# Setup of a cross-attention and expert kernel: query weights turned by transpositions, context loaded first

## The chip, the cores and the metric

The kernel runs on one core of a Trainium2 chip. The metric is the device time of one execution in microseconds, lower being better. One core has five engines that run side by side and meet only at semaphores: PE (TensorE, matrix products, with its weight loads listed as PEld), DVE (VectorE), ACT (ScalarE), POOL (GpSimd) and SP (SyncE, which here only starts transfers). All data are 32-bit floats.

## The reference

```python
x = x + xattn(ctx_1024, layernorm(x), fside, fside, ln1_w, ln1_b, ln2_w, ln2_b, Wq, Wkv, Wout)
x = x + ffn(layernorm(x), Wr, Wg, Wu, Wd)          # 9 experts, the best 2 for each token

def xattn(x, latents, shift, scale, ln1_w, ln1_b, ln2_w, ln2_b, Wq, Wkv, Wout):   # x: the context
    xn, ln = layernorm(x, ln1_w, ln1_b), layernorm(latents, ln2_w, ln2_b)
    q = ln @ Wq                                     # 16 heads of 64
    k, v = split(xn @ Wkv, 2)
    q = q * (1 + scale) + shift                     # one number for each batch and head
    attn = softmax(q . k / 8)                       # over the 77 context rows
    return (attn @ v) @ Wout
```

The input `x` is 4 x 1024 x 256, the context 4 x 77 x 256, `Wq` 256 x 1024, `Wkv` 256 x 2048, `fside` 4 x 16. The second layer norm has a weight `ln2_w` and an offset `ln2_b` for each of the 256 channels.

## The kernel before

The kernel has three stretches: a setup (to about 72 us in the trace), the attention of 32 groups of 128 tokens, and the experts. Only the setup is touched by the change. It folds everything that depends on the context alone into two tables, so that the attention needs no query projection. For each head, `g` = (query weights of the head) times (keys of the head): scores are then one product of normalised tokens with `g`. `u` does the same for values and `Wout`.

The schedule is manual (`tc.manual_schedule()`): each engine executes its instructions in the order of the program text. What is written first on an engine goes first, and an instruction that waits holds up all behind it on that engine. PSUM is used through `bank_tile`, which hands out eight banks in turn, so a product waits until the product eight places earlier has been read out. `evict(k, dst, src)` reads a bank out with DVE for odd k and with ACT for even k.

The setup's order around the change, with `P` = 128, `C` = 2 halves of the 256 channels, `NP` = 8 pairs of heads, `B * J` = 4 x 77 = 308 context rows:

- Lines 345 to 347: `qrows`, the two rows `ln2_w` and `ln2_b`, loaded from ACT's queue.
- Lines 367 to 374, SP's queue: `wq_sb` in four quarters of 256 KB with the context `cx` (308 KB) between the second and the third, then `wk_sb`, `wv_sb`, `wo_sb` of 1 MB each.
- Lines 376 to 389, POOL's queue: `cw`, `cb` (the weight and offset of the context's layer norm), `fs` (`fside` on all partitions), the router's weights, and the filling of `list_d` in DRAM.
- Lines 394 to 415: `fold`, a 256 x 256 matrix that is nearly diagonal. It holds `ln2_w` on the diagonal, and it also carries a subtraction of the last channel and the column of `ln2_b`, so that one product with it turns the query weights over (channels from partitions to the free dimension), scales them, and puts the offsets' product into the last column.
- Lines 417 to 427: moments of the context and `cn`, the normalised context, all on DVE but a root.
- `turn_queries(n)`, lines 431 to 438: for each pair of heads two products of `wq_sb` with `fold` into `pwq`, read out to `wqT`, by DVE and ACT in turn. Four pairs come ahead of the context's transpositions into `pct` (line 445, read out to `cT` at line 448 by ACT), four behind.
- Lines 456 to 466: `shift`, `scale1` from `fs`, on DVE.
- Lines 470 to 482: the key products `pk` (line 473), read out twice: to `kT` by ACT (477) and, times `scale1`, to `kTs` by DVE (478).
- Lines 483 to 489: `cfold`, small DVE products with the last column of `wqT`. Lines 493 to 509: the router's weights, with the product `pm`. Lines 535 to 553: small tables of numbers for the lists, on DVE.
- Lines 511 to 559, POOL: clearing of `vbd` (line 512, tied to the end of `normed`, the last write of `cn`), `vrem` and `u` (519, 521), and index patterns.
- Lines 560 to 573: 32 products `pgk` (line 565), one for each head and channel half. The two heads of a pair sit on different halves of the partitions. The first head of each pair is read out by ACT, the second by DVE, in two copies each.
- Lines 574 to 581: the products `pb`. Behind them, `kside` is given back, the first `x` are loaded, and the value side follows (`pwo`, `pv`, `pu`).

Of the kernel before, what the change touches and what calls it, by code (L numbers as in the profile page):

```python
# [8 lines left out]
F32 = mybir.dt.float32  # L9
# [12 lines left out]
def kernel(  # L22
# [319 lines left out]
    with tc.tile_pool(name="vside", bufs=1) as vside, ExitStack() as kvs:  # L342
        kside = kvs.enter_context(tc.tile_pool(name="kside", bufs=1))

        qrows = kside.tile([2, D], F32, name="qrows")
        for k, src in enumerate((ln2_w, ln2_b)):
            nc.scalar.dma_start(out=qrows[k : k + 1, :], in_=src.rearrange("(o d) -> o d", o=1))
# [19 lines left out]
        for k in range(4):  # L367
            if k == 2:
                nc.sync.dma_start(out=cx[:J], in_=ctx_in.rearrange("b j d -> j b d"))
            at = slice(k * quarter, (k + 1) * quarter)  # L370
            nc.sync.dma_start(out=wq_sb[:, :, at], in_=wq_v[:, :, at])
        nc.sync.dma_start(out=wk_sb, in_=wkv[:, :INNER].rearrange("(c p) n -> p c n", p=P))
# [4 lines left out]
        fs = vside.tile([P, B, NP, 2], F32, name="fs")  # L377
        nc.gpsimd.dma_start(
            out=fs.rearrange("p b n t -> p (b n t)"),
            in_=fside.rearrange("(o b) h -> o (b h)", o=1).to_broadcast([P, B * H]),  # L380
        )
# [9 lines left out]

        fold = kside.tile([P, C, D], F32, name="fold")
        minus = kside.tile([P, 1], F32, name="minus")
        nc.vector.memset(fold[:, 0, P:], 0.0)

        pq = bank_tile("pq")
        for c in range(C):
            nc.tensor.transpose(  # L400
                pq[:, 2 * c : 2 * c + 2], qrows[:, c * P : (c + 1) * P], ident[:2, :2]
            )
        qwb = kside.tile([P, C, 2], F32, name="qwb")
        nc.vector.tensor_copy(qwb.rearrange("p c k -> p (c k)"), pq[:, : 2 * C])
        qw = qwb[:, :, 0]
        nc.vector.tensor_scalar(fold[:, 0, :P], ident, qw[:, 0:1], None, ALU.mult)
        nc.vector.tensor_copy(fold[:, 0, D - 1 : D], qwb[:, 0, 1:2])
        nc.vector.scalar_tensor_tensor(
            minus, ident[:, P - 1 : P], -1.0, qw[:, 1:2], ALU.mult, ALU.mult
        )  # L410
        nc.scalar.activation(fold[:, 1, :P], ones, AF.Copy, scale=minus)
        nc.vector.tensor_scalar(
            fold[:, 1, P : D - 1], ident[:, : P - 1], qw[:, 1:2], minus, ALU.mult, ALU.add
        )
        nc.vector.tensor_copy(fold[:, 1, D - 1 : D], qwb[:, 1, 1:2])

        cmv = moments(cx[:J], J, "ctx")
        csd = kside.tile([P, B], F32, name="csd")
        cr = kside.tile([P, B], F32, name="cr")
        nc.scalar.activation(csd[:J], cmv[:J, :, 1], AF.Sqrt, bias=eps_t[:J])  # L420
        nc.vector.reciprocal(cr[:J], csd[:J])
        cn = kside.tile([P, B, D], F32, name="cn")
        for b in range(B):
            normed = nc.vector.tensor_scalar(
                cn[:J, b, :], cx[:J, b, :], cmv[:J, b, 0:1], cr[:J, b : b + 1],
                ALU.subtract, ALU.mult,
            )
        wqT = kside.tile([P, NP, D], F32, name="wqT")
        cT = vside.tile([P, C, B * J], F32, name="cT")

        def turn_queries(n):
            pt = bank_tile(f"pwq{n}")
            for c in range(C):
                nc.tensor.matmul(
                    pt[:, :D], wq_sb[:, c, n * P : (n + 1) * P], fold[:, c, :],
                    start=(c == 0), stop=(c == C - 1),
                )
            evict(n, wqT[:, n, :], pt[:, :D])

        for n in range(NP // 2):  # L440
            turn_queries(n)
        for c in range(C):
            pt = bank_tile(f"pct{c}")
            for b in range(B):
                nc.tensor.transpose(
                    pt[:, b * J : (b + 1) * J], cn[:J, b, c * P : (c + 1) * P], ident[:J, :J]
                )
            nc.scalar.activation(
                cT[:, c, :], pt[:, : B * J], AF.Identity,
                bias=cb[:, c : c + 1], scale=cw[:, c : c + 1],  # L450
            )
        for n in range(NP // 2, NP):
            turn_queries(n)
# [13 lines left out]

        kT = kside.tile([P, NP, B * J], F32, name="kT")
# [14 lines left out]
        for t in range(2):  # L483
            half = slice(64 * t, 64 * t + 64)
            nc.vector.tensor_tensor(
                cfold[half, :, t, :], scale1[half],
                wqT[half, :, D - 1 : D].to_broadcast([64, NP, B]), ALU.mult,
            )
            nc.vector.tensor_tensor(cfold[half, :, t, :], cfold[half, :, t, :], shift[half], ALU.add)
# [10 lines left out]
        pm = bank_tile("pm")  # L500
        for c in range(C):
            nc.tensor.matmul(pm[:, :E], ones, wr_sb[:, c, :], start=(c == 0), stop=(c == C - 1))
        nc.vector.tensor_tensor(
# [48 lines left out]
        for t, half in zip(nowhere, (lower, upper)):  # L552
            nc.vector.tensor_scalar(t, half, float(TOK), None, ALU.mult)
# [914 lines left out]
```

## Time and profile before

| | |
|---|---|
| median of 3 runs | 927.88 us (927.68 to 929.5) |
| the profiled execution's own time | 927.98 us, of which the span is 926.1 us |
| PE busy | 907.6 us, 98% of the span |
| DVE, ACT, POOL busy | 450.4, 339.2, 320.1 us |
| key products `pk` (line 473) | from 15.49, for 8.46 us |
| products `pgk` (line 565) | from 24.22 to 34.48 us |
| first value-side product `pwo` (line 607) | 35.59 us |

All times of single instructions are counted from the start of the span. A timeline line reads: start, time that the group covers, engine, line, operation, output <- inputs, shapes, count, and in brackets how long the engine had been idle before it and what ended the wait. Each product of 32-bit numbers appears as two MATMUL records, a transposition as one. Matmuls are pipelined, so the records overlap, and the distance between starts is the pace. In a table by stretches, each engine has its busy time and the number of instructions, and the last three columns are the clock that PE was granted, the share of the DMA engines, and GB/s.

### The profile page before, as it was taken

The numbers are of one execution on the slowest core, as the hardware profiler recorded it, in microseconds if no ns is written. First come the engines' busy times: TensorE is split into PE (matmuls) and PEld (weight loads), VectorE is DVE, ScalarE is ACT, GpSimd is POOL, SyncE is SP. The second block draws the span as 40 slices with busy tenths as digits, with TensorE's granted clock in tenths as the row PEclk, the third lists the DMA queues.
The fourth block names the chain that finished last, engine by engine and source line by source line (L and its number), as shares of the span: only waits on it lengthen the run. The fifth ranks groups of instructions, "written<-read, shape, count | busy, mean of one in ns | idle before, by whom it ended". The sixth has DMA issues, their size and how long they took to land. (4 is left out here: it accounts for less than half of the span.)

```text
span 926.1 us, 13326 instructions
## 1 busy us (share of the span) xinstructions
PE 907.6 (98%) x4190; PEld 706.7 (76%) x4190; DVE 450.4 (49%) x1330; ACT 339.2 (37%) x1071; POOL 320.1 (35%) x330
## 2 busy tenths in 40 slices
PE   8999999999999999999999999999999999999996
PEld 6676777777777777788887778777777777788885
DVE  5776678788788977753622222222222222222221
ACT  3567465665746565551111222222222211112210
POOL 5000000422504251246544444435435435444422
PEclk9999999999999999999999999999999999999998
DMA  6100010503112610455869779779779777779822
GB/s 211 47 23 1 1 69 24 46 24 46 34 36 69 222 36 24 117 143 157 204 188 305 212 207 308 216 207 308 219 209 311 223 211 217 221 220 308 233 34 23
DMA packets 109785, 136.92 MB, mean 148 GB/s; under 512 B 24251, under 2 KB 79939, under 8 KB 109716
## 3 DMA queue, kind: packets, MB, share of 16 engines
q1 hardware_dynamic: 92303, 118.78, 41.9%
q0 software_dynamic: 17408, 17.30, 10.5%
q8 instruction: 34, 0.56, 0.3%
q14 instruction: 36, 0.29, 0.1%
q10 hardware_dynamic: 4, 0.00, 0.0%
HBM read 119.38 MB, written 18.33 MB: 149 GB/s over the span
## 5 line engine op out<-in xcount | busy, mean ns | idle before, releaser
L1107 PE MATMUL pg<-xT,wgu 128*128 128x256 f32 x1144 | 251.7, 379 | 0.4 <-PEq L1424 0.4
L1107 PEld LDWEIGHTS pg<-xT,wgu 128*128 128x128 f32 x1144 | 215.9, 190 | 29.3 <-issue 0.8
L1181 PE MATMUL po<-wd,hid 128*128 128x256 f32 (+1 forms) x804 | 180.5, 379 | 0.0
L1181 PEld LDWEIGHTS po<-wd,hid 128*128 128x128 f32 (+1 forms) x804 | 147.2, 187 | 21.2 <-issue 0.7
L261 ACT ACTIVATE ex<-psc,mx 128x77 f32<-128x77 f32 x512 | 123.6, 360 | 102.0 <-DVE mx L251 102.0
L1216 POOL DMA_INDIRECT out_dram<-co,ids x63 | 100.7, 1598 | 172.1 <-DVE co L1184 148.3
L832 POOL DMA_INDIRECT list_d<-r_entry,r_pli x64 | 68.3, 1068 | 255.2 <-DVE r_pli L830 125.2
L324 PE MATMUL po<-u,aT 128*128 128x265 f32 x640 | 151.7, 391 | 0.9 <-ACT aT L313 0.6
L247 PE MATMUL psc<-g,zT 128*128 128x462 f32 (+1 forms) x384 | 139.1, 511 | 1.2 <-ACT zT L236 1.2
L324 PEld LDWEIGHTS po<-u,aT 128*128 128x128 f32 x640 | 118.7, 189 | 23.7 <-ACT aT L313 1.8
L1114 DVE TENSOR_TENSOR hid<-pg,sl 128x256 f32<-128x256 f32 x130 | 55.0, 424 | 160.2 <-ACT sl L1113 159.9
L1113 ACT ACTIVATE sl<-pg 128x256 f32<-128x256 f32 x130 | 49.7, 383 | 218.4 <-PE pg L1107 213.4
L247 PEld LDWEIGHTS psc<-g,zT 128*128 128x128 f32 x384 | 72.5, 189 | 59.2 <-issue 49.4
L1184 DVE TENSOR_SCALAR co<-po,ids 128x256 f32<-128x256 f32 x67 | 32.4, 484 | 136.4 <-PE po L1181 136.3
L1065 POOL DMA_INDIRECT yin<-y_d,ids x67 | 70.3, 1049 | 23.7 <-issue 17.3
L251 DVE TENSOR_REDUCE mx<-psc 128x6 f32<-128x462 f32 (+1 forms) x96 | 55.6, 580 | 18.4 <-PE psc L247 15.6
L281 DVE TENSOR_REDUCE sm<-ex 128x16 f32<-128x1232 f32 x32 | 45.9, 1435 | 36.9 <-ACT ex L261 36.3
L313 ACT COPY aT<-pa 128x512 f32<-128x512 f32 (+1 forms) x96 | 49.3, 551 | 27.2 <-PE pa L305 27.2
L305 PEld LDWEIGHTS pa<-ident,an 128*128 128x128 f32 x320 | 36.9, 141 | 7.7 <-PE po L324 1.4
L305 PE MATMUL pa<-ident,an 128*128 128x128 f32 x320 | 40.2, 273 | 1.0 <-DVE an L285 1.0
L285 DVE TENSOR_TENSOR an<-ex,rs 128x1024 f32<-128x1024 f32 x32 | 39.2, 1225 | 1.1
L1169 ACT COPY hid<-ph 128x384 f32<-128x384 f32 x15 | 7.2, 478 | 73.9 <-PE ph L1164 73.9
(305 smaller groups left out, 842.2 us busy)
## 6 DMA issues: line engine op xcount, KB each, us to landing
wgu<-in_L_ffn_Wg_dram SPq DMA_DIRECT2D x41, 704.0 KB
wd<-in_L_ffn_Wd_dram SPq DMA_DIRECT2D x41, 640.0 KB
wgu<-in_L_ffn_Wu_dram SPq DMA_DIRECT2D x41, 512.0 KB
wgu<-in_L_ffn_Wu_dram SPq DMA_DIRECT2D x41, 128.0 KB
x<-in_x_dram SPq DMA_DIRECT2D x8, 512.0 KB
out_dram<-x SPq DMA_DIRECT2D x8, 512.0 KB
y_d<-y SPq DMA_DIRECT2D x8, 512.0 KB
w<-in_L_ffn_Wg_dram SPq DMA_DIRECT2D x5, 704.0 KB
```

Source lines behind the costliest of these rows:

```text
L247: nc.tensor.matmul(psc[:, :w], zT[:, c, :], g_sb[i // NS // GPB][:, c, h * J : h * J + w], start=(c == 0), stop=(c == C - 1),)
L251: nc.vector.tensor_reduce(nmx[i][:, h : h + n], psc[:, : n * J].rearrange("p (h j) -> p h j", h=n), AX.X, ALU.max, negate=True,)
L261: nc.scalar.activation(exs[i][:, h + q, :], pscs[k][:, q * J : (q + 1) * J], AF.Exp, bias=nmx[i][:, h + q : h + q + 1],)
L305: nc.tensor.transpose(pa[:, q * P : (q + 1) * P], ans[i][:, (k + q) * P : (k + q + 1) * P], ident)
L324: nc.tensor.matmul(po[:, :DE], aT[:, n, :], u_sb[b][:, n, :], start=(n == 0), stop=(n == KC - 1))
L832: i = nc.gpsimd.indirect_dma_start(out=list_d[:, :], out_offset=bass.IndirectOffsetOnAxis(ap=place_i[:, s : s + 1], axis=0), in_=entries[k ...
L1065: return nc.gpsimd.indirect_dma_start(out=dst, out_offset=None, in_=src, in_offset=bass.IndirectOffsetOnAxis(ap=offsets, axis=0), **kw,)
L1107: nc.tensor.matmul(pg[:, g, :], w[:, c, at : at + P], xT[:, c, :], start=(c == 0), stop=(c == C - 1),)
L1113: nc.scalar.activation(sl, pg[:, 0, :], AF.Silu)
L1114: nc.vector.tensor_tensor(hid[:, f, :], pg[:, 1, :], sl, ALU.mult)
L1181: nc.tensor.matmul(po[rows, :D], hid[:, f, at], d[:, f, :], start=(f == 0), stop=(f == NF))
L1216: i = nc.gpsimd.indirect_dma_start(out=out_r, out_offset=bass.IndirectOffsetOnAxis(ap=rows_of(j, h, rows), axis=0), in_=cos[j][:, h, :], i ...
```

## The change

Four things are altered, all in the setup.

1. The query weights are turned by 16 plain transpositions (two pairs of heads to a bank) in place of 16 products with `fold`. `ln2_w`, now loaded on all partitions as `wrow`, is multiplied in when DVE reads the bank out (`scale_queries`, 128 x 512 at a time). The first of these comes ahead of `cT`, the other three each follow a key read-out. The subtraction of the last channel becomes eight ACT instructions in place, with `wlast`. `fold` and what built it is gone.
2. The product of the offsets `ln2_b` with the query weights is made by itself: `qb` holds the offsets in one column of 32, and 16 matmul records on four column tiles give `pcq`, which ACT copies to `crow`. `turn_offsets` turns it and makes `cfold`.
3. The context is loaded first, in two halves, ahead of the query weights; the key weights come in four quarters. `wrow` and `fs` are loaded from ACT's queue. Two of the four `cn` go to ACT, one of the two `cT` to DVE.
4. `turn_offsets`, `router_weights` and `numbers` are moved from ahead of the `pgk` loop into it, ahead of its pairs 2, 4 and 6.

```diff
-        qrows = kside.tile([2, D], F32, name="qrows")
-        for k, src in enumerate((ln2_w, ln2_b)):
-            nc.scalar.dma_start(out=qrows[k : k + 1, :], in_=src.rearrange("(o d) -> o d", o=1))
+        wrow = kside.tile([P, D], F32, name="wrow")
+        nc.scalar.dma_start(
+            out=wrow, in_=ln2_w.rearrange("(o d) -> o d", o=1).to_broadcast([P, D])
+        )
+        fs = vside.tile([P, B, NP, 2], F32, name="fs")
+        nc.scalar.dma_start(
...
-        for k in range(4):
-            if k == 2:
-                nc.sync.dma_start(out=cx[:J], in_=ctx_in.rearrange("b j d -> j b d"))
-            at = slice(k * quarter, (k + 1) * quarter)
-            nc.sync.dma_start(out=wq_sb[:, :, at], in_=wq_v[:, :, at])
-        nc.sync.dma_start(out=wk_sb, in_=wkv[:, :INNER].rearrange("(c p) n -> p c n", p=P))
+        for i in range(2):
+            at = slice(i * BH, (i + 1) * BH)
+            nc.sync.dma_start(out=cx[:J, at], in_=ctx_in[at].rearrange("b j d -> j b d"))
+        wk_v = wkv[:, :INNER].rearrange("(c p) n -> p c n", p=P)
+        for dst, src in ((wq_sb, wq_v), (wk_sb, wk_v)):
+            for k in range(4):
+                at = slice(k * quarter, (k + 1) * quarter)
+                nc.sync.dma_start(out=dst[:, :, at], in_=src[:, :, at])
...
-        fs = vside.tile([P, B, NP, 2], F32, name="fs")
-        nc.gpsimd.dma_start(
...
+        qb = kside.tile([P, C, P // QT], F32, name="qb")
+        nc.gpsimd.memset(qb, 0.0)
+        nc.gpsimd.dma_start(out=qb[:, :, 0], in_=ln2_b.rearrange("(c p) -> p c", p=P))
...
-        fold = kside.tile([P, C, D], F32, name="fold")
...
-        nc.vector.tensor_copy(fold[:, 1, D - 1 : D], qwb[:, 1, 1:2])
...
+        cm = kside.tile([P, B], F32, name="cm")
...
+        pwq = []
+        for n in range(0, NP, 2):
+            pt = bank_tile(f"pwq{n}")
+            for k in range(2):
+                for c in range(C):
+                    nc.tensor.transpose(
+                        pt[:, k * D + c * P : k * D + (c + 1) * P],
+                        wq_sb[:, c, (n + k) * P : (n + k + 1) * P], ident,
+                    )
+            pwq.append(pt)
...
+        def scale_queries(k):
+            nc.vector.tensor_tensor(
+                wqT[:, 2 * k : 2 * k + 2, :], pwq[k].rearrange("p (n d) -> p n d", n=2),
+                wrow.unsqueeze(1).to_broadcast([P, 2, D]), ALU.mult,
+            )
...
+        nc.vector.scalar_tensor_tensor(
+            cm[:J], cmv[:J, :, 0], -1.0, cr[:J], ALU.mult, ALU.mult
+        )
         cn = kside.tile([P, B, D], F32, name="cn")
         for b in range(B):
...
+            if b % 2:
+                normed = nc.vector.tensor_scalar(
...
+            else:
+                nc.scalar.activation(
+                    cn[:J, b, :], cx[:J, b, :], AF.Identity,
+                    bias=cm[:J, b : b + 1], scale=cr[:J, b : b + 1],
+                )
+        scale_queries(0)
         for c in range(C):
             pt = bank_tile(f"pct{c}")
...
+            if c:
+                nc.vector.tensor_scalar(
+                    cT[:, c, :], pt[:, : B * J], cw[:, c : c + 1], cb[:, c : c + 1],
+                    ALU.mult, ALU.add,
+                )
+            else:
+                nc.scalar.activation(
...
-        for n in range(NP // 2, NP):
-            turn_queries(n)
...
         for n in range(NP):
             pk = bank_tile(f"pk{n}")
...
+            if n < NP // 2 - 1:
+                scale_queries(n + 1)
+            elif n == NP // 2 - 1:
+                nc.vector.tensor_scalar(
+                    wlast, wqT[:, :, D - 1], -1.0, None, ALU.mult
+                )
+            if n >= NP // 2:
+                for m in (2 * n - NP, 2 * n - NP + 1):
+                    nc.scalar.activation(
+                        wqT[:, m, :], wqT[:, m, :], AF.Identity, bias=wlast[:, m : m + 1]
+                    )
+
+        pcq = bank_tile("pcq")
+        for c in range(C):
+            for q in range(QT):
+                nc.tensor.matmul(
+                    pcq[q * P // QT : (q + 1) * P // QT, :D], qb[:, c, :],
+                    wq_sb[:, c, q * quarter : (q + 1) * quarter],
+                    start=(c == 0), stop=(c == C - 1),
+                )
+        nc.scalar.copy(crow, pcq[:, :D])
+
+        def turn_offsets():
+            pt = bank_tile("pcqt")
+            for k in range(2):
+                nc.tensor.transpose(
+                    pt[:, k * P : (k + 1) * P], crow[:, k * P : (k + 1) * P], ident
+                )
+            nc.vector.tensor_copy(
+                cq.rearrange("p (q k) -> p q k", k=2),
+                pt[:, : 2 * P].rearrange("p (k q r) -> p q k r", k=2, q=QT)[:, :, :, 0],
+            )
...
+        def router_weights():
...
+        def numbers():
...
         for n in range(NP):
+            if n == 2:
+                turn_offsets()
+            if n == NP // 2:
+                router_weights()
+            if n == NP - 2:
+                numbers()
             for c in range(C):
```

## The prediction

> **What bounds the kernel now.** I read the busy table and the slices first.
>
> ```profile
> PE 907.6 (98%) x4190; PEld 706.7 (76%) x4190; DVE 450.4 (49%) x1330; ACT 339.2 (37%) x1071; POOL 320.1 (35%) x330
> ...
> PE   8999999999999999999999999999999999999996
> ```
>
> PE is full from the first slice on (23 us each) to the last. Whatever PE gains in the setup is passed on to the end, one for one, as nothing behind it waits for a fixed moment. So I follow PE's own timeline of the first 36 us:
>
> ```profile
> 4.44 6.46 PE L434 MATMUL pwq<-fold,wq_sb 128*128 128x256 f32 x16 [0.72 <-DVE fold L407]
> 10.74 1.42 PE L445 MATMUL pct<-ident,cn 77*128 77x77 f32 x8
> 11.99 3.66 PE L434 MATMUL pwq<-fold,wq_sb 128*128 128x256 f32 x16
> 15.49 8.46 PE L473 MATMUL pk<-cT,wk_sb 128*128 128x308 f32 x32
> ...
> 24.22 2.86 PE L565 MATMUL pgk<-kTs,wqT 64*128 64x308 f32 x18
> 28.03 6.45 PE L565 MATMUL pgk<-kTs,wqT 64*128 64x308 f32 x46 [0.96 <-DVE g L144]
> 34.42 1.24 PE L577 MATMUL pb<-kT,cfold 128*32 128x308 f32 x16
> 35.59 1.09 PE L607 MATMUL pwo<-ident,wo_sb 128*128 128x128 f32 x8
> ```
>
> The same product takes 6.46 us for the first sixteen records and 3.66 us for the second sixteen. The timeline of single stretches shows two paces:
>
> ```profile
> 6.31 1.06 PE L434 MATMUL pwq<-fold,wq_sb 128*128 128x256 f32 x2
> ...
> 12.25 0.59 PE L434 MATMUL pwq<-fold,wq_sb 128*128 128x256 f32 x2
> ```
>
> The starts are 0.43 us apart in the first and 0.22 in the second. The distance changes at 9.8 us, 5.3 after the first dense product. PE starts slow and becomes twice as fast; the granted clock stands at 1.00 all the while. Next DVE and POOL, from the timelines of these engines:
>
> ```profile
> 7.91 1.40 DVE L163 BATCH_NORM_STATS2 bn_ctx<-cx 77x6 f32<-77x256 f32 x4 [3.01 <-DMA cx<-in_ctx_dram]
> ...
> 15.95 1.94 POOL L521 MEMSET u<- 128x1060 f32 x2
> ...
> 16.03 1.89 DVE L460 COPY shift<-fs 64x32 f32<-64x32 f32 x2
> ...
> 27.36 7.71 DVE L144 COPY g<-pgk 128x154 f32<-128x154 f32 x32
> ```
>
> The context lands only at 7.9. The two tiny copies of 64x32 last 0.94 us each, exactly as long as POOL's two memsets beside them: a copy within SBUF waits for the POOL instruction that is running. And DVE reaches its read-outs of `pgk` at 27.36, as small work holds it from 24.8 on; PE, eight banks ahead, stands still for it before 28.03. Last, the table by stretches for the transfers:
>
> ```profile
> 4.00:5.50 1.50, 1.06 (x3) 0.88 (x4) 0.82 (x5) 0.40 (x1) 1.50 (x3) 1.00 0.51 103
> ...
> 7.00:8.50 1.50, 1.50 (x5) 1.15 (x5) 0.59 (x2) 0.00 (x0) 0.00 (x0) 1.00 1.28 304
> 8.50:9.00 0.50, 0.50 (x3) 0.41 (x2) 0.50 (x3) 0.00 (x0) 0.00 (x0) 1.00 0.71 180
> 10.00:14.00 4.00, 3.92 (x22) 3.03 (x22) 2.21 (x8) 1.93 (x5) 2.40 (x1) 1.00 1.01 412
> ```
>
> Query weights and context are 1.36 MB, with the small loads 1.42. Adding up the GB/s of the half microseconds gives 1.47 MB at 8.5, a part of it the filling of `list_d`. The dip after 8.5 and the rise to 412 mark the passage to the key weights with their longer rows. So the last query quarter lands at about 8.7 now.
>
> **The change part by part.** Counted against the profiled execution: 927.98 us, its span 926.1. That is 0.1 above the median.
>
> *Loads.* Ahead of the last query quarter stand the same bytes, in another order, and 0.13 MB for `wrow`. At the 304 GB/s of the third row this is 0.4 us; where engines stand half idle, as in the first row, it is nothing. Bounds 8.6 to 9.7; I take 9.0. SP issues 12 transfers where it issued 8, at 0.47 us each; the next on its queue is `x` at 35, so this is free. ACT issues two, as before. POOL gives up one issue (0.57) and gets one with a small memset: its last issue at 6.6 still ends ahead of `vbd`, which waits for `cn`. The first key quarter (256 KB, 0.9 us at 1 KB rows) lands at 9.9, about 1.5 us before it is needed; without that cover each microsecond would count in full.
>
> *Up to the key products.* PE's order is: sixteen transpositions, eight of the context, keys. The transpositions replace 10.1 us of PE time. The first twelve follow their quarters; only the last four count. Nearest row: `pwo`, eight in 1.09 us, so 0.12 each at full pace, 0.23 at the slow one: 0.5 to 0.9. The eight of `pct`, whose last five took 0.55 in all, 0.09 apart, cost 0.7 at the slow pace for the four that count; then 0.25 to drain and 0.55 for ACT's `cT`. Keys start at 9.0 + 0.9 + 0.7 + 0.25 + 0.55 = 11.4 at the slow pace, 10.7 at the full one, against 15.49. The context is no longer late: landed by 4 to 6, then 2.7 us of statistics, root and scaling, so `cn` is done by 8.5. If it landed 1.5 us later than that it would set the start. The steps that built `fold` (DVE, 3.8 to 4.9) lay ahead of an idle DVE; taking them out gives nothing.
>
> *The pace.* This decides. 32 key records take 8.46 us at full pace, 0.264 each, and 0.514 at the slow one (times 0.427/0.219). By the trace alone any work could be what brings PE up to speed: PE then counts as busy from the first quarter on (about 6 us), has its 5.3 us at 11.3 and runs the keys at full pace. Against this stands the Trainium skill, "TensorE: Matmul & The Clock Gate", Part 4, PE-mode transpose: transpositions do not count as activity for the clock gate. By Part 1 of that page the switch comes after one full window of about 3.4 us of matmul activity, and windows run freely, so 3.4 to 6.8 us after dense work begins; the 5.3 of the trace lies inside. The change takes away just the dense matmuls that used up the slow time, and hands it to the keys. The skill's rule gives: switch at 11.4 + 5.3 = 16.7, by then 10.3 records; 21.7 more at 0.264 are 5.7; keys end at 22.4 against 23.95, a gain of 1.55. With the switch 3.4 or 6.8 us after the start it is 2.5 or 0.8. The trace's reading leaves PE to be paced by DVE (below), which ends the keys at 21.0, a gain of 2.9. No row shows transpositions on a slow PE, so I take the rule.
>
> *DVE behind `cT`.* The shift work of 16.03 to 18.88 comes at about 11.6 now, and POOL's memsets (6.4 us from the end of `cn`, so 8 to 14.4) run beside it. Four instructions, each held to the end of a POOL instruction of 0.95: the first `kTs` ends at about 15.0, bounds 12.6 (no hold at all) and 15.5. Then `scale_queries` (128x512; from 0.42 for 128x256 and 0.48 for 308, about 0.65 in a row) and `kTs` (0.42) alternate: the last bank of `pwq` comes free at 17.75. The sixth key product needs that bank. With slow keys it starts at 19.3, so 1.5 us of cover; with fast ones it would start at 16.1 and waits.
>
> *ACT.* Eight instructions in place (0.37 by the 128x256 read-outs, bounds 0.3 and 0.5) and `kT` (0.41) for the last four keys: 1.15 us a key against PE's 1.06. A lag of 0.4 builds up; with `crow`, ACT is free 0.9 us after `pcq`, when the first `pgk` is ready. Free.
>
> *`pcq`.* 16 records on column tiles: `pb` had 16 in 1.17 up to the next start at 308 columns, so 0.97 at 256. On PE's path. Bounds 0.6 and 1.2. Its `qb`, issued by 4, would land like `fs` (7.4 us) or `list_d` (8.1) at about 12, ten before it is read. `pm` (0.45) leaves this place and comes back in the loop.
>
> *The loop.* PE's own work there is 64 records at 0.132 (two heads side by side: 8.45), with two transpositions 0.28 and `pm` 0.45: 9.2. It took 10.2, since DVE came late. DVE's read-outs take 0.48 for each of 16 pairs of products; PE needs 0.53. The work moved into the loop is 1.0 (copy and four `cfold` steps), 0.5 and 1.15 us ahead of pairs 4, 8, and 12. Stepping through it with eight banks: DVE falls behind by 1.0, catches nothing up, and ends 2 us behind PE's last product, but never by more than the four pairs that PE may be ahead; PE waits about 0.25 at `pb`. From the end of the keys to `pwo`: before 35.59 - 23.95 = 11.64; after 0.97 + 9.2 + 1.17 + 0.25 = 11.6. Zero; with one bank less than I count it costs 0.5.
>
> Sum: 927.9 - 1.55 - 0.05 = 926.3.
>
> **The rivals.** 0.2% is 1.86 us, about what measurements of this kernel can tell from no change.
>
> A, the forecast: the slow time moves to the keys. 926.3, own range 925.3 to 927.6.
>
> B: transpositions do bring PE up to speed. Keys start at 10.7 and DVE's chain ends them at 21.0: 925.0. For it speaks that with quarters arriving every 0.9 us, four slow transpositions keep PE nearly busy; against it the rule above.
>
> C: B, and the shift work slips between POOL's memsets. The keys end at 10.8 + 8.46 = 19.3: 923.3. The rows at 16.03 speak against it.
>
> D: the last query quarter lands at 9.7 and DVE's backlog costs 0.5 in the loop: 927.6. Then the change does little of what it says, for PE's saved work was hidden behind the load.
>
> E, slower: PE stays at the slow pace all through the keys, as the stream in front of it has too many holes. The keys then take 16.4 us and end at 27.8: 3.85 later, 931.8. It decides from a switch later than 19.6 us: then half of the keys are slow and the gain is gone. Against it: slow keys are dense, as slow PE is their only bound, and the trace's dense stretch switched after 5.3.
>
> **How the numbers follow.** A 0.55, B 0.27, C 0.06, D 0.07, E 0.05. Over 0.2% faster: 0.4 of A, nearly all of B, C: 0.53. Within: the rest of A and B, D: 0.42. Slower: E, 0.05. The range takes in B with half a microsecond, A and D: 924.4 to 928.0; outside are C, E and edges, about 15%.
>
> **What would show it.** In the changed profile, the 32 key records should start at 11 to 11.7 with starts 0.51 apart, falling to 0.26 at 15 to 18. Starts of 0.26 from the beginning mean B. `cx` should be read by DVE before 6. The shift copies should last as long as POOL's memsets. `pcq` should take about 1 us, and PE should not idle over 0.5 in the loop. I am wrong if `pwo` starts later than 35.6, or if the keys wait for `wk_sb` or for `cT` at a time well beyond 12.

## The result, and the profile after

The changed kernel takes 925.86 us in the median (925.18 to 927.51, nine runs), beside 928.46 for the kernel before on the same chip (927.68 to 930.42, nine runs). The ratio is 0.9968, with a 95% interval from 0.9959 to 0.9977: 2.6 us or 0.3% faster. Timed once more on another chip (`timed` below) the ratio is 0.9973 [0.9961, 0.9984]. The forecast was 926.3.

The profiled execution was the slowest of its nine: 927.51 us, of which the span is 925.8. Its busy table and slices look like those of before:

```profile
PE 904.9 (98%) x4190; PEld 702.2 (76%) x4190; DVE 450.6 (49%) x1325; ACT 341.3 (37%) x1076; POOL 319.6 (35%) x331
...
PE   6999999999999999999999999999999999999996
```

Only the first slice differs, a 6 for an 8: PE now begins later. PE's timeline of the setup, with the columns of the one before:

```profile
7.10 4.22 PE L417 MATMUL pwq<-ident,wq_sb 128*128 128x128 f32 x16 [7.10 <-DMA wq_sb<-in_L_xattn_Wq_dram]
11.12 1.24 PE L452 MATMUL pct<-ident,cn 77*128 77x77 f32 x8
12.54 10.19 PE L485 MATMUL pk<-cT,wk_sb 128*128 128x308 f32 x32 [0.18 <-ACT cT L461]
22.66 1.07 PE L512 MATMUL pcq<-wq_sb,qb 128*32 128x256 f32 x16
23.66 2.35 PE L626 MATMUL pgk<-kTs,wqT 64*128 64x308 f32 x16
25.93 0.44 PE L522 MATMUL pcqt<-ident,crow 128*128 128x128 f32 x2
26.30 2.34 PE L626 MATMUL pgk<-kTs,wqT 64*128 64x308 f32 x16
28.57 0.61 PE L553 MATMUL pm<-wr_sb,ones 128*128 128x9 f32 x4
29.12 4.42 PE L626 MATMUL pgk<-kTs,wqT 64*128 64x308 f32 x32
33.47 1.24 PE L638 MATMUL pb<-kT,cfold 128*32 128x308 f32 x16
34.64 1.09 PE L668 MATMUL pwo<-ident,wo_sb 128*128 128x128 f32 x8
```

The keys begin 2.95 us earlier than before (12.54 for 15.49). They last 10.19 us where they lasted 8.46, and end 1.22 earlier (22.73 for 23.95). `pwo` begins 0.95 earlier (34.64 for 35.59). DVE and POOL beside it:

```profile
5.37 1.61 DVE L402 BATCH_NORM_STATS2 cst<-cx 77x6 f32<-77x256 f32 x4 [3.72 <-DMA cx<-in_ctx_dram]
...
12.91 1.16 DVE L471 COPY shift<-fs 64x32 f32<-64x32 f32 x2
...
13.03 1.97 POOL L574 MEMSET u<- 128x1060 f32 x2
...
14.11 0.93 DVE L473 TENSOR_SCALAR scale<-shift 128x32 f32<-128x32 f32 x1
...
24.52 2.10 DVE L144 COPY g<-pgk 128x154 f32<-128x154 f32 x8 [0.55 <-PE pgk L626]
```

The context is read 2.5 us earlier. Two of the tiny shift steps (the second copy, 0.94 us by itself, and the scale) still last as long as POOL's memsets beside them. And DVE now waits for `pgk` where PE waited for DVE.

The trace also records the clock granted to PE, as entries with a start. The first entry of full pace stands at 10.02 us before and at 15.86 after. Ahead of its first entry a trace has none, and the views print 1.00 there. PE's busy time in the two stretches of 3.41 us ahead of 15.86, and in the last one ahead of 10.80 in an execution whose setup is the same up to there (`loop_back` below), is the first thing to read (columns: stretch and length, PE busy and records, PEld, DVE, ACT, POOL, clock, DMA share, GB/s):

```profile
9.03:12.45 3.42, 3.19 (x17) 2.56 (x16) 0.25 (x2) 0.65 (x2) 3.42 (x2) 1.00 1.09 355
12.45:15.86 3.41, 3.32 (x7) 2.26 (x8) 3.33 (x8) 0.45 (x2) 3.41 (x6) 1.00 1.04 398
```

```profile
7.39:10.80 3.41, 3.40 (x16) 2.60 (x15) 1.58 (x5) 1.10 (x3) 2.30 (x1) 1.00 1.12 302
```

In `loop_back` the stretch ahead of the switch holds the real transpositions alone, and PE was busy in it for 3.40 of 3.41 us. In the changed kernel's execution the stretch with the transpositions had holes of 0.23 us, and PE became fast only after the next stretch, which the keys filled.

### The profile page after: what moved, and what is told of

The parts are those of the page before. It is cut to its first block, busy times and chain, and to the rows that moved or that the text cites. A ratio compares the mean times of both kernels' runs of the same rounds, so it can differ in the third digit from the quotient of the medians.

```text
span 925.8 us, 13336 instructions
## 1 busy us (share of the span) xinstructions
PE 904.9 (98%) x4190; PEld 702.2 (76%) x4190; DVE 450.6 (49%) x1325; ACT 341.3 (37%) x1076; POOL 319.6 (35%) x331
```

## The experiments

All of them together first. "Full pace from" is the first entry of full clock in the trace; the four times are those of the profiled execution, in us. A kernel is compared with the kernel before on its own chip.

| kernel | median (range, runs) | ratio to before, 95% | full pace from | keys start | keys end | `pwo` |
|---|---|---|---|---|---|---|
| before | 927.71 to 928.77 by chip | 1 | 10.02 | 15.49 | 23.95 | 35.59 |
| after | 925.86 (925.18–927.51, 9) | 0.9968 [0.9959, 0.9977] | 15.86 | 12.54 | 22.73 | 34.64 |
| `again` | 926.53 (1) | | 16.14 | 12.74 | 22.97 | 34.88 |
| `timed` | 925.86 (925.57–926.63, 7) | 0.9973 [0.9961, 0.9984] | 16.59 | 12.56 | 23.10 | 35.02 |
| `warm_turns` | 924.30 (923.35–925.35, 5) | 0.9962 [0.9949, 0.9976] | 5.96 | 11.77 | 21.26 | 33.17 |
| `warm_products` | 924.81 (924.41–925.15, 6) | 0.9967 [0.9955, 0.9979] | 6.74 | 11.93 | 21.28 | 33.18 |
| `before_turns` | 928.97 (926.95–932.81, 13) | 1.0009 [0.9998, 1.0020] | 5.00 | 19.45 | 27.91 | 39.56 |
| `old_loads` | 928.68 (927.71–929.32, 21) | 1.0009 [1.0002, 1.0015] | 19.10 | 13.94 | 25.04 | 36.95 |
| `ctx_first` | 928.81 (927.59–930.89, 12) | 1.0000 [0.9991, 1.0009] | 10.81 | 16.22 | 24.68 | 36.33 |
| `loop_back` | 927.23 (925.38–928.22, 20) | 0.9980 [0.9973, 0.9987] | 10.80 | 12.02 | 21.86 | 35.14 |
| `loop_only` | 927.00 (924.82–928.37, 18) | 0.9987 [0.9980, 0.9994] | 11.89 | 16.43 | 24.89 | 35.23 |
| `quiet_act` | 927.11 (926.19–930.02, 13) | 0.9989 [0.9980, 0.9999] | 11.10 | 12.16 | 25.19 | 37.10 |
| `tuned` | 923.37 (923.07–923.89, 5) | 0.9944 [0.9931, 0.9958] | 5.72 | 11.39 | 19.92 | 31.84 |
| `tuned2` | 924.98 (924.22–926.88, 5) | 0.9964 [0.9950, 0.9977] | 6.46 | 11.64 | 20.20 | 32.11 |

### The same kernel again

`again` and `timed` are the changed kernel without an edit, for further traces of it.

> The changed kernel as it is, for a second profile. Theory A (the slow pace of PE is moved onto the key products, and when it ends is a matter of chance, 3.4 to 6.8 us after they begin): the last query quarter again lands near 10.2, the keys begin near 12.5, but the distance between their starts falls from 0.51 to 0.26 at another moment than 15.9, somewhere between 15.9 and 19.3. Theory C (the transfers differ from execution to execution): the keys begin a microsecond or more earlier than 12.5, and that is why the median lies 1.6 under the profiled execution. If the late gathered rows near 715 us (0.64) were all that was special about the first profile, this one ends 0.6 earlier and the setup looks the same.

> The changed kernel as it is, timed beside the other three. The first query quarter lands near 7.1 and the keys begin near 12.6, as in both profiles so far; the median is 925.9 within 0.7. The switch of PE to full pace falls anywhere from 3.3 to 6.8 us after the keys begin, so single executions spread over about 1.7 us.

All three traces begin the keys at 12.5 to 12.7 and switch to full pace at 15.9 to 16.6, inside the keys. The setup ends earlier than before by 0.95, 0.71 and 0.57 us at `pwo`. That is less than the 2.6 and 2.9 us by which the medians differ; I come back to this.

### Do transpositions bring PE up to speed?

The first is the question on which the prediction chose a rule. `warm_turns` puts 28 transpositions of a constant tile on PE while it waits for the first query quarter:

```diff
+        warm = bank_tile("warm")
+
+        def spin(count):
+            for _ in range(count):
+                nc.tensor.transpose(warm[:, :P], warm_in[:, :P], ident)
+
+        spin(28)
         pwq = []
```

> The changed kernel with 28 dense transpositions (128x128, never read) on PE from 1.5 us, the same 6 us of PE time at the slow pace as the seven products of the run before, none between the quarters. Theory A (transpositions do not count): they and the real ones all start 0.21 apart, the keys begin slow at 0.51, and the time is that of the changed kernel, 925.9 within 0.5. Theory B (any work brings PE up to speed, and in the changed kernel it only had too many holes): starts go to about 0.12 by 8 us, the keys run at 0.26 from the first, and the time is that of the run with products, 924.4.

PE's timeline of `warm_turns`:

```profile
1.45 5.46 PE L418 MATMUL warm<-ident,warm_in 128*128 128x128 f32 x28 [1.45 <-POOL ident masks.py:199]
7.19 0.66 PE L426 MATMUL pwq<-ident,wq_sb 128*128 128x128 f32 x4 [0.28 <-DMA wq_sb<-in_L_xattn_Wq_dram]
...
11.77 3.38 PE L494 MATMUL pk<-cT,wk_sb 128*128 128x308 f32 x12 [0.43 <-ACT cT L470]
15.43 5.83 PE L494 MATMUL pk<-cT,wk_sb 128*128 128x308 f32 x20 [0.29 <-DVE cfold L485]
```

Nothing but transpositions ran on PE ahead of 5.96, where full pace begins. They count. Two single stretches of the same run show it without the clock entry: five records cover 1.27 us in the first and seven cover 0.93 in the second.

```profile
4.71 1.27 PE L418 MATMUL warm<-ident,warm_in 128*128 128x128 f32 x5
...
5.98 0.93 PE L418 MATMUL warm<-ident,warm_in 128*128 128x128 f32 x7
```

`warm_products` does the same with 7 products of 128x256 (14 records), and one more behind each of the first three quarters.

> The changed kernel with seven dense products (128x256, never read) on PE from 1.5 us, while it would wait for the query weights, and one more after each of the first three quarters. Theory A (PE comes up to speed through matrix products only, and the keys pay for it in the changed kernel): the transpositions and all keys run at full pace, starts 0.26 apart from the first key; the keys then wait for DVE's chain and end near 21.8 against 22.7; 0.8 us faster than the changed kernel where its switch came early, about 1.5 in the median, so 924.4. Theory B (PE was not really slow for this reason, or the keys are bound by something else): no change, 925.9.

Full pace from 6.74, and the rest as in `warm_turns` within 0.2 us. In both, the keys are fast from their first record and still last 9.4 to 9.5 us, not 8.46: they wait for DVE's chain of read-outs, and end at 21.3 (`tuned` below moves that chain). The prediction's case B had 21.0.

`before_turns` gives the kernel before the same help: nine such transpositions ahead of `pq` and three behind it.

> The kernel before with nothing but twelve transpositions added on PE (128x128, never read), nine from 1.5 us and three while PE waits for fold. Theory (PE's slow start costs the kernel before too, and transpositions count towards the full pace): the switch comes 3 us earlier than the 10.0 of the first profile, on average, between 4.9 and 8.3; each microsecond saves half: 1.5 us faster than before. Rival (the page's rule that transpositions do not count): switch at 7.9 to 11.3 as before, no change.

This fell. PE was fast from 5.00, ended the first half of the fold products 2.3 us earlier (8.6 for 10.9), and then had nothing to do, since the context had not landed. PE's timeline, its waits, and the table by stretches:

```profile
4.69 3.91 PE L441 MATMUL pwq<-fold,wq_sb 128*128 128x256 f32 x16
11.65 1.87 PE L452 MATMUL pct<-ident,cn 77*128 77x77 f32 x8 [3.05 <-DVE cn L431]
13.32 6.30 PE L441 MATMUL pwq<-fold,wq_sb 128*128 128x256 f32 x16
```

```profile
PE pct L452 <- DVE cn L431: 3.1, 1, 3.1
```

```profile
8.42:11.83 3.41, 0.36 (x2) 0.14 (x1) 2.50 (x11) 0.82 (x3) 0.00 (x0) 1.00 1.01 365
11.83:15.24 3.41, 3.38 (x13) 2.63 (x13) 1.40 (x5) 1.12 (x2) 2.62 (x1) 0.50 1.03 401
15.24:18.66 3.42, 3.42 (x10) 2.70 (x9) 0.42 (x1) 0.37 (x1) 3.42 (x4) 0.50 0.75 246
```

After a stretch with 0.36 us of work the clock stands at 0.50 for 6.83 us (11.83 to 18.66), which covers the second half of the fold products but for its last microsecond. So in this trace the want of pace was not what held the kernel before: with the context that late, a faster PE waits and then loses its pace. This execution took 932.81 us where the median is 928.97, so it shows the mechanism and not its usual price; the median says that on the whole nothing is gained.

### Is it the load order, or the transpositions?

`old_loads` is the changed kernel with the context back between the second and the third query quarter:

```diff
-        for i in range(2):
-            at = slice(i * BH, (i + 1) * BH)
-            nc.sync.dma_start(out=cx[:J, at], in_=ctx_in[at].rearrange("b j d -> j b d"))
...
             for k in range(4):
+                if dst is wq_sb and k == 2:
+                    nc.sync.dma_start(out=cx[:J], in_=ctx_in.rearrange("b j d -> j b d"))
                 at = slice(k * quarter, (k + 1) * quarter)
```

> The changed kernel with the load order of before on SP's queue: two query quarters, the whole context, two query quarters, then the key quarters. Theory A with the forecast's reading of the loads: the first query quarter lands by 4.4 in place of 7.1 and the last near 9 in place of 10.2, but the context lands at 7.9 in place of 5.4, so that its transpositions come near 10.8 and the keys begin near 12.3: no change within 0.5, 925.9. Rival (context first is what brings the gain): the keys begin at 13.5 or later, 927 or more. Rival (context first costs, as it delays the query weights that are needed first): the keys begin by 11.5, 924.9.

`ctx_first` is its counterpart, the kernel before with nothing but the load order of the changed one:

```diff
-            if k == 2:
-                nc.sync.dma_start(out=cx[:J], in_=ctx_in.rearrange("b j d -> j b d"))
...
+        for i in range(2):
+            at = slice(i * B // 2, (i + 1) * B // 2)
+            nc.sync.dma_start(out=cx[:J, at], in_=ctx_in[at].rearrange("b j d -> j b d"))
```

> Kernel before with the load order of the changed kernel alone: the context in two halves first, then the query weights, the key weights in quarters; fold and its products stay. Theory (the load order pays only together with the transpositions): the first query quarter lands at 7.0, as in the kernel with fside and the weights on other queues, so the dense products begin at 7 and not at 4.4, the switch to full pace comes at about 11 to 12, sixteen records are done at 12.9, the other sixteen at 17.2; keys start at 17.3 (before 15.5), pwo at 37.2 (before 35.6), time 1.5 us over the kernel before. Rival 1 (the load order brings the gain by itself): 926, keys at about 14. Rival 2 (the products are paced by the loads on both sides): no change, keys at 15.5 to 16.

Either part without the other gains nothing: the ratios are 1.0009 and 1.0000. They are not yet like for like, since `old_loads` has the small work in the loop and `ctx_first` has not. That move alone gives 0.9987 (`loop_only` below), and the changed kernel without it gives 0.9980 (`loop_back` below). So the load order alone is worth nothing (1.0000). The whole change without the loop's part, which is load order and transpositions together, is worth 0.9980. And the transpositions in the order of before lose (1.0009, where the loop's part alone has 0.9987). PE's timelines, first of `old_loads`, then of `ctx_first`:

```profile
7.26 2.32 PE L416 MATMUL pwq<-ident,wq_sb 128*128 128x128 f32 x8 [7.26 <-DMA wq_sb<-in_L_xattn_Wq_dram]
10.52 1.97 PE L416 MATMUL pwq<-ident,wq_sb 128*128 128x128 f32 x8 [0.94 <-DMA wq_sb<-in_L_xattn_Wq_dram]
...
13.94 11.10 PE L484 MATMUL pk<-cT,wk_sb 128*128 128x308 f32 x32 [0.18 <-ACT cT L460]
```

```profile
6.55 5.79 PE L436 MATMUL pwq<-fold,wq_sb 128*128 128x256 f32 x16 [2.57 <-DVE mv_ctx L165]
...
16.22 8.46 PE L475 MATMUL pk<-cT,wk_sb 128*128 128x308 f32 x32
```

In `old_loads` the context in the middle delays the last two query quarters, PE stands idle for 0.94 us among the transpositions, and the switch comes only at 19.10. The prediction's case E set its limit at 19.6, and this run is next to it. Of what was expected, the rival with 927 or more and keys at 13.5 or later held.

This run undoes the order only. `wrow` and `fs` stay on ACT's queue, and the first query quarter, though first in SP's, landed at 7.12, not by 4.4 as expected; in before's trace it landed at 3.85. From 2.0 to 4.0 us SP's queue moved 77 rows of 1 KB here and 477 before. What the transpositions do with all the loads as before was not run.

In `ctx_first` the dense products begin 2.1 us later than before, at 6.55 (the row names DVE as what ended the wait, but the first query quarter landed just ahead, at 6.42), but full pace comes 4.3 us behind their start and not 5.6, and only 0.73 us of the delay reaches the keys. I expected 1.5 us more; the number of the second rival, no change, is the one that holds. The span of that run (929.0) is longer for another reason, told under "One for one" below.

### The small work in the loop

`loop_back` takes the changed kernel and calls `turn_offsets`, `router_weights` and `numbers` ahead of the `pgk` loop:

```diff
+        turn_offsets()
+        router_weights()
+        numbers()
         for n in range(NP):
-            if n == 2:
-                turn_offsets()
-            if n == NP // 2:
-                router_weights()
-            if n == NP - 2:
-                numbers()
```

> The changed kernel with turn_offsets, router_weights and numbers called ahead of the loop again, all else as changed. Theory (the move is what brought 0.4 to 0.9 us, by letting DVE read out the first products at once): DVE reaches its first read-out 2.7 us later, at about 26.7, PE stands still once for 0.6 to 1.0 us after its ninth product, but the two gaps of 0.25 around the moved transpositions and the router's product are not won back, as they stay on PE's path: 926.5, 0.6 slower than the changed kernel. Rival (the move only shifts DVE's work about): no change.

Its median is 1.4 us over that of `timed` on the same chip; by the ratios it is 0.7 us, with intervals that overlap. Its PE and DVE rows:

```profile
23.65 0.44 PE L522 MATMUL pcqt<-ident,crow 128*128 128x128 f32 x2 [0.79 <-ACT crow L517]
...
27.56 6.48 PE L623 MATMUL pgk<-kTs,wqT 64*128 64x308 f32 x44 [0.33 <-DVE g L144]
...
26.97 7.65 DVE L144 COPY g<-pgk 128x154 f32<-128x154 f32 x32
```

PE waits for `crow` and then for DVE, which begins its read-outs at 26.97 instead of 24.52. From the end of the keys to `pwo` it takes 13.28 us, against 11.91 in the changed kernel. `loop_only` is the other direction: the kernel before, with just its `cfold` steps, router's weights and numbers moved into the loop, and no other edit.

> The kernel before with one part of the change alone: the small steps of cfold, the router's weights and the number tables are moved into the loop, ahead of its pairs 2, 4 and 6; loads and query weights stay as before. Theory (letting DVE read out the first products at once is a good half of the gain; taking the move back from the changed kernel cost 1.4 in the median): PE's wait of 0.96 at 28.0 is gone, pm costs 0.25 more inside the loop, and the first value-side product comes at about 34.8 in place of 35.6; 0.8 to 1.4 faster than the kernel before. Rival (DVE's work is only shifted and comes back as a wait at the end of the loop): no change, within 0.3.

By the ratio it is 1.2 us faster than before [0.6, 1.9], by the medians 0.8. From the end of the keys to `pwo` it takes 10.34 us against 11.64, and PE's rows have no wait left there. Its keys began 0.9 later in this execution, since `qrows` landed at 4.38 instead of 3.39, which no edit touched. So moving the small work is worth 1.3 to 1.4 us in the traces from either side, a part of which is the wait for `crow` in `loop_back`, and about 1 us in the times. Of the parts tried alone it is the only one that pays by itself.

### Versions that might be better

`quiet_act` moves the broadcast loads away from ACT's queue: `wrow` to SP behind the query weights, `fs` to POOL. The reason was that in the changed kernel only 111 rows of 1 KB moved on SP's queue between 2.0 and 4.0 us, against 477 before.

> The changed kernel with the two broadcast loads taken off ACT's queue: wrow goes on SP's queue behind the four query quarters, fs on POOL's, where it was before. Theory (the two broadcast loads on ACT's queue hold up the rows of SP's queue in the first microseconds: between 2.0 and 4.0 us SP's queue moved 477 rows of 1 KB in the kernel before and 111 in the changed one): the first query quarter lands by 5.5 in place of 7.1, the last by 9 in place of 10.2, the keys begin near 11.4, the time is 1.2 less than that of the changed kernel, 924.7. Rival (the context's rows, on 11 of 16 DMA engines, are what is slow): the first query quarter still lands near 7, no change.

The rows came back (428), the context landed at 3.6, but PE could take up the last query quarter only at 10.04 (10.21 in after). The theory fell: its median, 927.11, is 1.2 us over that of `timed` beside it. In its trace (928.88 us) a new wait shows. POOL's clearing, tied to `cn`, now begins at 7.82 (8.69 in after), and DVE's copies meet it at 12.28. DVE and PE rows, and the stretches around the wait:

```profile
12.28 4.16 DVE L472 COPY shift<-fs 64x32 f32<-64x32 f32 x2
...
18.22 6.97 PE L486 MATMUL pk<-cT,wk_sb 128*128 128x308 f32 x20 [2.68 <-DVE wqT L428]
```

```profile
14.51:17.93 3.42, 1.03 (x4) 0.40 (x3) 3.34 (x7) 0.83 (x2) 1.70 (x23) 1.00 1.06 376
...
17.95:21.30 3.35, 3.08 (x6) 2.19 (x7) 2.29 (x6) 0.41 (x1) 0.00 (x0) 0.50 0.97 362
```

Two copies of 64x32 take 4.16 us, and the first alone 3.97. It ends at 16.25, just behind the last of POOL's setup instructions (16.21), after more than twenty of them in a row. In after the same copies met the same clearing and took 0.21 and 0.94; why they came through there and not here is not shown. The bank of `pwq` comes free that much later, PE idles for 2.68 us in front of the keys' second part, and its clock falls to half for one stretch.

`tuned` draws the conclusion. The 28 transpositions of `warm_turns` stay, `fs` comes on SP's queue right behind the context and `wrow` behind the query weights, and the shift and scale steps stand ahead of DVE's reciprocal, so ahead of `cn` and of all that POOL does behind it:

```diff
+        nc.sync.dma_start(
+            out=fs.rearrange("p b n t -> p (b n t)"), ...
...
+        for t in range(2):
+            half = slice(64 * t, 64 * t + 64)
+            nc.vector.tensor_copy(shift[half], fs[half, :, :, t].rearrange("p b n -> p n b"))
...
         nc.vector.reciprocal(cr[:J], csd[:J])
```

> The changed kernel with 28 dense transpositions on PE from 1.5 us (never read), fs on SP's queue behind the context, wrow on SP's queue behind the query quarters, and the shift and scale steps of DVE moved ahead of the root's read-out, before POOL's memsets begin. Theory (three things held the keys: the query weights' late landing, the slow pace, and DVE's steps held by POOL's memsets): last query quarter by 9, keys from 10.6 all with starts 0.26 apart and no wait, key products over at 19.1 against 22.7 in the changed kernel and 21.2 with the transpositions alone; 922.3. Rival (another engine takes over): keys over at 20.5 or later, 923.5 or more.

PE and DVE:

```profile
11.39 8.53 PE L495 MATMUL pk<-cT,wk_sb 128*128 128x308 f32 x32 [0.61 <-DMA wk_sb<-in_L_xattn_Wkv_dram]
...
31.84 1.09 PE L678 MATMUL pwo<-ident,wo_sb 128*128 128x128 f32 x8
...
5.80 0.83 DVE L446 COPY shift<-fs 64x32 f32<-64x32 f32 x2 [0.63 <-DMA fs<-in_fside_Bx_dram]
```

The keys now have one length, 8.53 us, with no wait inside. `pwo` begins 3.75 us earlier than before, and the median is 923.37, the best of all: ratio 0.9944, though its interval overlaps that of `warm_turns`. The 922.3 expected was not reached, as the keys began at 11.39 and not at 10.6. This is the prediction's case C (keys end 19.3, 923.3), reached by an edit that the change does not have.

`tuned2` puts `wrow` behind the first key quarter, since `tuned` waits 0.61 us for the key weights, and the first `scale_queries` behind `cT`.

> The version called tuned with two further changes of order: wrow is loaded behind the first key quarter, not ahead of it, and DVE's first scale_queries comes behind its cT. In the profile of tuned the keys waited 0.61 for the first key quarter, and cT on DVE stood behind the read-out that needs wrow. Theory: the keys begin at 10.9 in place of 11.4 and nothing else moves, 922.9. Rival (the first key quarter is limited by all the bytes ahead of it, and wrow is a small part): under 0.2 faster, 923.3.

A miss. The wait for `wk_sb` is gone, yet the keys begin 0.25 later, as the first query quarter landed later in this execution (7.92 on PE). In the same execution (926.88 us, median 924.98) a single wait of 2.2 us for ACT's `xT` in the experts took most of the lead that was left. The intervals of `tuned` and `tuned2` overlap, so which is better is not settled.

## Why the prediction was right, and where not

**Right in the total and in its main case.** Case A said that the slow time moves into the keys: begun slow, switch between 15 and 18, end 1.55 earlier. The traces show 0.51 us between starts at first, the switch at 15.86, and an end 1.22 earlier.

**Loads: the mis-sized term.** The last query quarter was put at 9.0 with an upper bound of 9.7; it landed at 10.17. The mistake lies already in the reading of before: I took the dip in GB/s after 8.5 for the landing, but in that trace the slowest of the sixteen engines ends its part of the quarter at 10.29. In after, fifteen engines were done at 9.98 and the last at 10.17, and PE took up the quarter at 10.21: the slowest engine decides, which a sum of GB/s cannot show. The change left this landing where it was: three traces with the loads of before have 10.10 to 10.55, and six with those of the changed kernel 10.01 to 10.37. (`ctx_first` has 9.13; which of its loads makes the difference was not tried.) From the landing to the keys I had 2.4 us and it took 2.37, so the whole 1.14 us of delay at the keys' start (12.54 for 11.4) is this term.

**The pace: the rule failed, the number stood.** I took from the Trainium skill ("TensorE: Matmul & The Clock Gate", Part 4, PE-mode transpose) that transpositions do not count for the clock. `warm_turns` contradicts it: full pace at 5.96 after nothing but transpositions. The trace's own reading, "any work counts", was the right one. The forecast came out all the same because the real transpositions wait for their quarters, and that was luck. In all fourteen traces full pace first came after a stretch of 3.41 us in which PE was busy for 3.25 us or more (3.25 in `quiet_act`, 3.32 in after, 3.40 or more in the others), and it did not come after stretches with 3.03 to 3.23 (after, `again`, `timed`, `old_loads`). The real transpositions are right at that edge: full pace from 10.80 in `loop_back` and 11.10 in `quiet_act`, not yet in the other four. (The busy share is not all: after its fall, `before_turns` stayed slow past a stretch with 3.38, and `quiet_act` rose after one with 3.12. What else decides is open.) A and B are thus not two theories but two outcomes of one mechanism. The length of the stretches agrees with Part 1 of the same page (windows of about 3.4 us): all entries of the traces, but those cut off by the end, are multiples of 3.41 us long (3.41, 6.83, and so on to 904.53, which is 265 of them). Where I gave 5.3 us from dense keys to full pace, it took 3.3, 3.4 and 4.0. So the keys lasted 10.2 to 10.5 us where the forecast had 11.0, which won back 0.5 to 0.8 us of the late start.

**B's price.** An early switch brings `pwo` to 33.17 (`warm_turns`), 1.5 us earlier than after; the prediction had 1.3 between A and B, and named what stops it, the chain on DVE behind POOL's memsets. In `tuned`, which moves that chain and the two loads it begins with, the keys have no wait left.

**DVE behind `cT`, ACT, `pcq`.** Two of the four shift steps were held for 0.93 us or more, where I had all four; the first `kTs` ended 3.4 us behind the keys' start, forecast 3.6. `pcq` took 1.0 (forecast 0.97). ACT never ended a wait of PE behind the keys' first product.

**The loop.** Forecast 9.2 and a wait of 0.25, so 9.45; measured 9.81 (23.66 to 33.47), with no wait. DVE, at 24.52 for its first read-out, was in time. Instead the two insertions take 0.37 and 0.55 from start to next start (forecast 0.28 and 0.45), and each run of products between them is 0.13 to 0.16 longer than its 0.132 a record, as 2.27 for the first sixteen shows. Together this is 0.6 over 8.45 + 0.28 + 0.45. From the keys' end to `pwo` it was 11.91 instead of 11.6.

**"Zero" for the loop hid two terms.** `pcq` costs 1.0, and the moved work gives back about 1.3 (in the traces). The prediction named the sum; that this move is the part that pays alone came only from `loop_only` and `loop_back`.

**The share of each part.** No case of the prediction was that load order and transpositions are worth nothing alone and pay together. In the traces each is held up without the other: an early context is of no use while the fold products keep PE busy (to 16.2 in `ctx_first`), and with the context in the middle the transpositions, short as they are, wait for the query quarters behind it (landed at 10.48 and 11.14 in `old_loads`, at 8.91 and 10.17 in after). The order is not the whole of that wait: before had the same order and 8.52 and 10.29, without the broadcast loads on ACT's queue.

**"One for one".** PE's lead over the kernel before, instruction by instruction, was 0.95 us at `pb` in the profiled execution of after and 0.89 ahead of the experts' first gathered rows at about 416 us (`again` 0.71 and 0.71, `timed` 0.57 and 0.54). So up to there the lead is passed on nearly whole. Then it changes: 1.36 behind these rows and 0.33 at the end in after; 1.3 and 1.5 at the end in `again` and `timed`. The largest steps are waits for gathered rows (`yin`). These are PE's waits for them near 417 us, in before, after and `tuned`:

```profile
PE px L1093 <- DMA yin<-y_d,ids: 1.4, 1, 1.4
```

```profile
PE px L1154 <- DMA yin<-y_d,ids: 0.9, 1, 0.9
```

```profile
PE px L1164 <- DMA yin<-y_d,ids: 0.7, 2, 0.5
```

In `timed` the wait is 0.4 us, and `loop_only` and `warm_turns` have none. The prediction said that nothing behind the setup waits for a fixed moment, and these waits do not contradict it: with a fixed moment a kernel that comes earlier would wait longer, but `tuned`, 4.0 us ahead there, waits less than before does, and `warm_turns`, 2.4 ahead, not at all. What it did not foresee is that the wait differs between executions by up to 2.0 us, more than the setup's gain. In `ctx_first` PE waited 2.0 us there, and that had a consequence:

```profile
416.00:420.40 4.40, 2.37 (x15) 1.87 (x15) 2.01 (x9) 1.16 (x3) 3.22 (x6) 1.00 0.93 277
420.50:423.80 3.30, 3.30 (x10) 2.58 (x9) 0.00 (x0) 0.03 (x1) 1.22 (x2) 0.50 1.01 340
```

The clock fell to half for one stretch, 400 us away from the setup, and the lead went from -0.81 to -2.88. What the medians gain beyond the setup's 0.57 to 0.95 us, 1.6 to 2.3 us, no trace accounts for. That such waits are shorter, or falls of the clock rarer, in the changed kernel would fit, but no run shows it. It would fit as well that before's setup often ends later than in its one trace: `loop_only`, whose code is the same up to the keys, began them at 16.43 and not at 15.49. It stays open. The agreement of 926.3 with 925.86 is therefore in part luck: the setup's part, forecast at 1.6, was half of that in the traces.

## What to carry to other kernels

Ask of a slow stretch in front of a kernel what it covers: a PE that starts early, or becomes fast early, is of use only if the next operand is there, and if it is not, the idle time can cost the pace as well. Parts of a change that are worth nothing one by one, as load order and transpositions here, can pay together, so undo them one at a time from the full change, not only add them to the old kernel. Small work on an engine that is about to become the consumer of a loop belongs between the loop's steps, not ahead of it.

## What the runs showed of the hardware

- Plain transpositions of 32-bit data raise PE's pace as products do: full pace 4.5 us after the first of 28 in `warm_turns`, 5.4 us after the first product in `warm_products`.
- The pace is decided in stretches of 3.41 us. Stretches with 0.36, 1.03 and 1.38 us of PE's work (`before_turns`, `quiet_act`, and 417.00 to 420.41 in `ctx_first`) were followed by half pace for 6.83, 3.41 and 3.41 us. Stretches with 1.97 (before, 416.21 to 419.62) and 2.21 (`tuned2`, 436.54 to 439.95, around its wait of 2.2 us) were not. So a wait of 2.0 us can cost the pace and one of 2.2 not, by how it lies to the stretches.
- A DVE copy within SBUF can be held over many POOL instructions in a row, not just to the end of the running one: 3.97 us for one copy of 64x32 in `quiet_act`, to the end of the last of them.
- With broadcast loads on ACT's queue at the start, SP's queue moved fewer rows (111 in after against 477 in before, of 1 KB, from 2.0 to 4.0 us). Moving them away brought the rows back (428 in `quiet_act`) but not the last query quarter (landed at 9.99 for 10.17).
